# One number per unit instead of a maximum per query: the shift of the scores moves from TensorE into the exponential's bias

## The chip, the cores and the metric

One core of a Trainium2 chip. The metric is device time in microseconds; the kernel before took 1728.9 us (median of 3 runs, 1727.37 to 1731.29). TensorE (PE) multiplies, VectorE (DVE) adds and reduces, ScalarE (ACT) does the exponentials and copies, GpSimd (POOL) issues the adding DMAs, SyncE (SP) issues the other DMAs, each in its own order.

## The reference

A pre-norm block over x of shape (2, 2048, 512): 16 query heads of width 32 in 2 key groups, rotary positions, and then a feed-forward product in emulated 8-bit floats. The part that matters here is the attention:

```python
q = q * cos + rotate_half(q) * sin
q = q * hd ** (-0.5)
k = k * cos + rotate_half(k) * sin
scores = jnp.einsum('bqhd,bkhd->bhqk', q, k_exp) * hd ** (-0.5)
attn = jax.nn.softmax(scores, axis=-1)
out = jnp.einsum('bhqk,bkhd->bqhd', attn, v_exp).reshape(b, s, d)
return out @ wo + bo
```

A softmax is the same whatever number is taken from all scores of one query, as long as the exponentials and their sum stay in range.

## The kernel before, in words

**Units and rounds.** The attention is 64 units of 256 queries by 4 heads. A unit goes over its 2048 keys in 16 chunks of 128, four chunks to a round, so four rounds to a unit (r = 0 to 3). Scores stand as [128 keys, 4 heads x 256 queries] in one of two PSUM tiles `T` (E and O, two banks each); even chunks use one, odd chunks the other. Keys are kept as the difference to the key 256 places earlier (`dkS`), so a chunk's matmuls add to what the tile already holds, and the tile then holds the chunk's own scores.

**A chunk** (`probabilities`, L1008): two matmuls of 512 columns into `T` (L1022), then one exponential of 128x1024 on ACT (L1031) into a tile `p`. Chunk c can start on PE only when the exponential of chunk c - 2 has read the tile.

**The shift before.** For chunks 0 and 1 of a unit, four matmuls of 256 columns (L1013, `sel` against `maxima`) first put minus the maximum of each query into the tile. These maxima come from `first_scores` (L514), called for the next unit at the ends of rounds 0 and 1: four matmuls of 128 columns (L523) give the scores of 128 queries by 128 keys, and DVE reduces them to one maximum per query and head (L531). In round 2 DVE splits the maxima into two parts (L504, L505). In round 3 `gather_maxima` (L538) turns them around with two PE transposes (L543) and copies them to `mT` on ACT (L547).

**The order inside a round** is written out by hand (L1075 on): chunks c0 and c1; DVE adds their two `p` (L1005); PE multiplies the four `p` of the round before with the values (`columns`, L968, 32 matmuls, called by `weigh`); up to two pieces of other work from job queues (`fill`); in round 3 DVE adds two earlier sums (L1038, `join`) and the maxima are gathered; chunks c2 and c3; their DVE addition and a POOL DMA that adds the other pair onto it (L1035); in rounds 0 and 1 `first_scores` of the next unit; one or two more pieces (`fill`), mostly one matmul of a projection (L295) each. The jobs are projections, rotary positions, norms and outputs of other blocks.

**The SP queue** carries the loads of x, keys and queries in program order. A query projection ends in an ACT copy (L439) and, on SP, eight DMAs of 32 KB that swap halves of heads (`sw_q`, L308); the rotated queries are written to DRAM (`q_far`, L469) and read back stacked (`qst`, L349).

**Ends.** `finish_heads` (L934) copies the sums with ACT (L939) and takes their reciprocal as exp(-ln) (L942, L943). At the end of the kernel the largest sum is compared with a bound; if it is over it, or not a number, a slow general path runs (from L1391).

Of the kernel before, what the change touches and what calls it, by code (L numbers as in the profile page):

```python
# [8 lines left out]
F32 = mybir.dt.float32  # L9
F32R = mybir.dt.float32r  # L10
BF16 = mybir.dt.bfloat16
U32 = mybir.dt.uint32
AF = mybir.ActivationFunctionType
ALU = mybir.AluOpType
AX = mybir.AxisListType

P = 128
HEADS = 16
GROUPS = 2
HD = 32  # L20
TB = 512
NT = TB // P
EPS = 1e-5
E4M3_MAX = 448.0
# [3 lines left out]
def preln_attn_fp8_ffn_kernel(  # L28
# [57 lines left out]
    AV_BANKS = 2  # L86
    FIRST = P
    MOST_BITS = float(0x5D5E0B6B)

    const = ctx.enter_context(tc.tile_pool(name="const", bufs=1))  # L90
    xpool = ctx.enter_context(tc.tile_pool(name="x", bufs=3))
# [90 lines left out]
    ones = const.tile([P, HD], F32, tag="ones", name="ones")  # L182
    nc.gpsimd.memset(ones, 1.0)

    sel = const.tile([P, 4, P], F32R, tag="sel", name="sel")
    nc.gpsimd.memset(sel.bitcast(F32), 0.0)
    for j in range(4):
        nc.gpsimd.memset(sel[j * HD : j * HD + 2, j, :].bitcast(F32), -1.0)
    mrow = const.tile([P, HB], F32R, tag="mrow", name="mrow")
    nc.gpsimd.memset(mrow.bitcast(F32), 0.0)  # L190


    def layernorm_stats(src, mean, rstd, name, tiles=range(NT)):
# [17 lines left out]
    def quantized_scale(amax, scale, inv, name):  # L211

        across = bank(f"across_{name}")
        nc.tensor.transpose(across[:1, :P], amax, ident)
        whole = small.tile([1, 1], F32, tag="whole", name=f"whole_{name}")
        nc.vector.tensor_reduce(whole, across[:1, :P], AX.X, ALU.max)
        give_back()
        down = bank(f"down_{name}")

        nc.tensor.matmul(down[:, :1], sel[:1, 0, :].bitcast(F32), whole, start=True, stop=True)  # L220
        nc.vector.tensor_scalar(scale, down[:, :1], -1.0 / E4M3_MAX, 1e-12, ALU.mult, ALU.max)
        give_back()
        nc.vector.reciprocal(inv, scale)

# [269 lines left out]
    def group(k):  # L494
        return quads[k][1] // (QUADS // GROUPS)

    split = []
    largest = {}

    def split_maxima():  # L500

        if split:
            mview, mx = split.pop()
            nc.vector.tensor_copy(mview[:, :, :, 0], mx)  # L504
            nc.vector.tensor_tensor(  # L505
                mview[:, :, :, 1], mx, mview[:, :, :, 0].bitcast(F32), ALU.subtract
            )

    def first_scores(u, i):  # L514

        k, half = units[u]
        if i == 0:
            largest[u] = small.tile([P, HT, 4], F32, tag="mx", name=f"mx_{u}")
        mx = largest[u]
        s = ps_s.tile([P, 4, FIRST], F32, tag="s0", name=f"s_{u}_{i}")  # L520
        at = (half * HT + i) * P
        for j in range(4):
            nc.tensor.matmul(  # L523
                s[:, j, :],
                qst[k][:, j, at : at + P],
                stacked["dkS"][:, group(k), :FIRST],
                start=True,
                stop=True,
                skip_group_check=True,
            )  # L530
        nc.vector.tensor_reduce(mx[:, i, :], s, AX.X, ALU.max)  # L531
        if i == HT - 1:
            mview = mrow.rearrange("p (i j r) -> p i j r", i=HT, j=4)
            split.append((mview, largest.pop(u)))

    maxima = {}

    def gather_maxima(u):  # L538

        split_maxima()  # L540
        tp = ps_s.tile([P, TB], F32, tag="s0", name=f"mtp_{u}")
        for i in range(HT):
            nc.tensor.transpose(  # L543
                tp[:, i * P : (i + 1) * P], mrow[:, i * P : (i + 1) * P].bitcast(F32), ident
            )
        mT = wide.tile([P, HB], F32R, tag="mT", name=f"mT_{u}")
        nc.scalar.copy(mT, tp[:, :HB])  # L547
        maxima[u] = mT


    mean2 = const.tile([P, NBLK, NT], F32, tag="mean2", name="mean2")
# [123 lines left out]
    def run(steps):  # L675
        for _ in steps:
            pass
# [14 lines left out]
    def first(steps, n):  # L692

        for _ in range(n):
            if next(steps, "end") == "end":
                return
            yield
# [4 lines left out]
    with tc.manual_schedule():  # L702
# [22 lines left out]

        run(first(kv[3], FRONT))
        run(prepare_weight(w_all))
        for i in range(HT):
            first_scores(0, i)
        run(first(kv[3], MIDDLE))  # L730
        gather_maxima(0)
        run(kv[3])


    attending[0] = True
# [70 lines left out]
        return 2 if r >= 2 and owed > (ROUNDS + r - 2) * left else 1  # L806

    seen = const.tile([P, len(units)], F32, tag="seen", name="seen")
    without_x = {}
    x_res = {}  # L810
    x_taken, x_done = [], set()
# [111 lines left out]
    def ask(u):  # L923

        k, half = units[u]
        n, quad = quads[k]
        if n == NBLK - 1 and quad == 3 and half == 0:

            fetch_y(4, wide, "qst", bufs=2)
            fetch_y_over_keys(5, "dkS", 0)  # L930
# [3 lines left out]
    def finish_heads(u, both, sums):  # L934
# [4 lines left out]
        nc.scalar.activation(total, sums, AF.Copy, accum_out=seen[:, u : u + 1])  # L939
        yield LATER  # L940
        yield ON_DVE
        nc.scalar.activation(guess, total, AF.Ln)  # L942
        nc.scalar.activation(guess, guess, AF.Exp, scale=-1.0)  # L943
        yield LATER
# [63 lines left out]
    def probabilities(u, T, kc):  # L1008

        k, half = units[u]  # L1010
        if kc < 2:
            for j in range(4):
                nc.tensor.matmul(  # L1013
                    T[:, j, :],
                    sel[:, j, :],
                    maxima[u],
                    start=(j % 2 == 0),
                    stop=True,
                    skip_group_check=True,
                )  # L1020
        for j in range(0, 4, 2):
            nc.tensor.matmul(  # L1022
                T[:, j : j + 2, :],
                stacked["dkS"][:, group(k), kc * P : (kc + 1) * P],
                qst[k][:, j : j + 2, half * HB : (half + 1) * HB],
                start=False,
                stop=True,
                skip_group_check=True,
            )
        p = ppool.tile([P, 4, HB], F32, tag="p", name=f"p_{u}_{kc}")  # L1030
        nc.scalar.activation(p, T, AF.Exp, scale=SCALE)  # L1031
        return p

    def accumulate(to, of):
# [23 lines left out]
    with tc.manual_schedule():  # L1058
        behind = None
        before = None  # L1060
        for u, (k, half) in enumerate(units):
# [13 lines left out]
            for r in range(ROUNDS):  # L1075
# [3 lines left out]
                    landing.pop()()  # L1079
                if r == 2:  # L1080
                    ask(u)
                load_wanted(u)
                load_some()
                last = r == ROUNDS - 1
# [13 lines left out]
                        Job(finish_heads(before.u, before.both, before.avs[:, 1, :]))  # L1098
                    )
                fill(ON_DVE, 2)  # L1100
                if r == 2:
                    split_maxima()
                if last:
                    join(unit.far[1], unit.far[0])
                    if u + 1 < len(units):
                        gather_maxima(u + 1)

                probs.append(probabilities(u, banks[0], chunks[2]))
                probs.append(probabilities(u, banks[1], chunks[3]))
# [4 lines left out]
                if before and r == 1 and in_two(before.u):  # L1114
                    join(before.far[3], before.far[2])
                behind = unit, chunks, probs
                if r < HT and u + 1 < len(units):
                    first_scores(u + 1, r)
                fill(ON_PE, pieces(u, r, ending_soon))
                fill(ON_DVE, 2)  # L1120
# [78 lines left out]
            multiplied(n, i, ready)  # L1199
            ready = ahead  # L1200

    top = small.tile([P, 1], F32, tag="top", name="top")
    nc.vector.tensor_reduce(top, seen.bitcast(U32), AX.X, ALU.max)
    across = bank("across_seen")
    nc.tensor.transpose(across[:1, :P], top, ident)
    flag = small.tile([1, 1], mybir.dt.int32, tag="flag", name="flag")
    nc.vector.tensor_reduce(top[:1], across[:1, :P], AX.X, ALU.max)
    nc.vector.tensor_scalar(flag, top[:1], MOST_BITS, None, ALU.is_gt)
    over = nc.values_load(flag, min_val=0, max_val=1)


# [259 lines left out]
```

## Time and profile before

| what | value |
| --- | --- |
| runs | 1728.9 us median (1727.37 to 1731.29) |
| the profiled execution's own time | 1724.88 us |
| its span | 1723.0 us |
| mean granted TensorE clock | 0.975 |
| exponentials (L1031) | 1024, 992.6 us busy, 1024 ns each |
| `sel` matmuls (L1013) | 512, 94.5 us busy |
| matmuls of the first scores (L523) | 512, 72.8 us busy |
| transposes of the maxima (L543) | 128, 28.0 us busy |
| reductions of the first scores (L531) | 128, 87.5 us busy |

The span runs from the profiled execution's first instruction to its last. A group's busy time is the union of its instructions; matmuls overlap in the pipeline, so that their mean duration is longer than the pitch at which they are issued. "Idle before" is the time for which the engine stood still just ahead of the group, with what ended it. PE is its matmuls and PEld its weight loads; SPq is SP issuing DMAs.

### The profile page before, as it was taken

To read this page: it belongs to the slowest core of one execution; us is meant where nothing else is said; L and a number is where in the kernel's file an instruction comes from. 1 tells how busy PE (TensorE), PEld (TensorE's weight loads), DVE (VectorE), ACT (ScalarE), POOL (GpSimd) and SP (SyncE) were. 2 spreads that over 40 slices of the span, in tenths; PEclk is the share of its full clock that TensorE was granted. 3 is DMA by queue.
4 is the path that set the end of the run, shared out by engine and by line. 5 is a ranking of instruction groups with operands and counts; after the bars stand their busy time and mean duration, and the time that the engine had idled before them with its cause. 6 is when DMAs were issued, how large, how long until landed. Compare 5 with 4: busy or idle time off the path is not lost.

```text
span 1723.0 us, 33241 instructions
## 1 busy us (share of the span) xinstructions
PE 1575.1 (91%) x13483; PEld 900.6 (52%) x13483; DVE 1248.8 (72%) x1673; ACT 1236.4 (72%) x1629; POOL 317.1 (18%) x381
## 2 busy tenths in 40 slices
PE   5499999999999999999999999999999989999565
PEld 2255555555555555555555555555555555555222
DVE  4447677677887769776877687767777686676697
ACT  2257877777777777777777777877777777777375
POOL 3321112211212112211221122111211122111100
PEclk9699999999999999999999999999999999999888
DMA  6657769867778767878786688656867597576222
GB/s 203 201 122 178 170 146 216 195 127 160 184 178 164 183 153 160 192 147 195 175 196 134 118 199 177 152 117 154 184 149 154 105 203 145 116 187 138 56 86 112
DMA packets 105810, 272.61 MB, mean 158 GB/s; under 512 B 15920, under 2 KB 16560, under 8 KB 102960
## 3 DMA queue, kind: packets, MB, share of 16 engines
q0 software_dynamic: 41328, 142.10, 44.2%
q1 hardware_dynamic: 61904, 126.92, 25.3%
q8 instruction: 108, 1.77, 0.4%
q10 hardware_dynamic: 2416, 1.38, 0.3%
q14 instruction: 54, 0.44, 0.1%
HBM read 87.36 MB, written 40.89 MB: 74 GB/s over the span
## 4 chain that ended last, share of the span: by engine, by line
PE 67%; DVE 10%; DMA 8%; issue 7%; ACT 5%; SPq 2%; POOL 1%; ACTq 0%; DVEq 0%; POOLq 0%
PE avs L968 23%; PE T L1022 23%; PE po L295 5%; ACT p L1031 5%; PE pq L295 4%; PE T L1013 3%; PE avs L986 3%; PE s L523 2%; DMA pa<-pa 2%; DMA qst<-q_far 2%; PE pk L295 2%; PE mtp L543 1%; DVE v L236 1%; DVE pa L1005 1%; DMA sw_q<-q 1%
## 5 line engine op out<-in xcount | busy, mean ns | idle before, releaser
L1031 ACT ACTIVATE p<-T 128x1024 f32<-128x1024 f32 x1024 | 992.6, 1024 | 178.3 <-PE T L1022 171.1
L1005 DVE TENSOR_TENSOR pa<-p,p 128x1024 f32<-128x1024 f32 x511 | 624.7, 1223 | 356.1 <-ACT p L1031 355.0
L1022 PE MATMUL T<-qst,dkS 128*128 128x512 f32 x2048 | 680.0, 442 | 24.8 <-ACT p L1031 23.8
L968 PE MATMUL avs<-p,vX 128*32 128x256 f32 x8192 | 495.1, 382 | 0.0
L1022 PEld LDWEIGHTS T<-qst,dkS 128*128 128x128 f32 x2048 | 338.7, 188 | 273.6 <-ACT p L1031 153.5
L1035 POOL DMA_DIRECT2D pa<-pa x255 | 221.0, 867 | 1201.2 <-DVE pa L1005 915.3
L968 PEld LDWEIGHTS avs<-p,vX 128*32 128x32 f32 x8192 | 239.9, 109 | 225.8 <-issue 93.9
L1038 DVE TENSOR_TENSOR pa<-pa,pa 128x1024 f32<-128x1024 f32 x125 | 152.3, 1219 | 16.0 <-DMA pa<-pa 15.9
L295 PE MATMUL po<-wo_sb,attn 128*128 128x512 f32 x256 | 129.6, 603 | 0.0
L295 PE MATMUL pq<-xnT_q,wq_sb 128*128 128x512 f32 x224 | 111.8, 601 | 0.0
L1013 PE MATMUL T<-mT,sel 128*128 128x256 f32 x512 | 94.5, 307 | 6.5 <-ACT p L1031 6.1
L1013 PEld LDWEIGHTS T<-mT,sel 128*128 128x128 f32 x512 | 72.9, 188 | 46.9 <-ACT p L1031 30.8
L986 PE MATMUL avs<-pa,ones 128*32 128x256 f32 x1048 | 80.7, 382 | 11.9 <-DVE pa L1038 11.1
L531 DVE TENSOR_REDUCE mx<-s 128x4 f32<-128x512 f32 x128 | 87.5, 683 | 2.8 <-PE s L523 2.8
L1056 ACT COPY both<-avs 128x256 f32<-128x256 f32 x64 | 23.9, 373 | 86.7 <-PE avs L986 86.7
L523 PEld LDWEIGHTS s<-dkS,qst 128*128 128x128 f32 x512 | 77.2, 192 | 14.7 <-DVE mx L531 3.1
L939 ACT ACTIVATE both<-avs 128x256 f32<-128x256 f32 x64 | 24.6, 385 | 71.7 <-PE avs L986 71.7
L523 PE MATMUL s<-dkS,qst 128*128 128x128 f32 x512 | 72.8, 265 | 2.2 <-DVE mx L531 2.1
L295 PEld LDWEIGHTS po<-wo_sb,attn 128*128 128x128 f32 x256 | 44.3, 190 | 17.6 <-issue 11.0
L986 PEld LDWEIGHTS avs<-pa,ones 128*32 128x32 f32 x1048 | 27.8, 109 | 43.7 <-DVE pa L1038 30.4
L295 PEld LDWEIGHTS pq<-xnT_q,wq_sb 128*128 128x128 f32 x224 | 39.4, 190 | 17.4 <-issue 13.5
L1171 PE MATMUL xtp<-ident_bf,xq 128*128 128x128 bf16 x128 | 16.0, 266 | 34.3 <-DVE xq L237 34.3
(128 smaller groups left out, 1033.0 us busy)
## 6 DMA issues: line engine op xcount, KB each, us to landing
pa<-pa POOLq DMA_DIRECT2D x255, 512.0 KB, 5.2
qst<-q_far SPq DMA_DIRECT2D x128, 256.0 KB, 7.0
q_far<-hi_q SPq DMA_DIRECT2D x32, 256.0 KB, 4.6
q_far<-lo_q SPq DMA_DIRECT2D x32, 256.0 KB, 4.5
x_res<-in_L_attn_x_dram SPq DMA_DIRECT2D x16, 512.0 KB, 10.8
x_res<-in_L_attn_bo_dram POOLq DMA_DIRECT2D x32, 256.0 KB, 6.7
out_dram<-v SPq DMA_DIRECT2D x16, 512.0 KB, 2.8
sw_q<-q SPq DMA_DIRECT2D x240, 32.0 KB, 3.1
```

Of the source, the lines that this page charges most:

```text
L295: nc.tensor.matmul(dst, lhs(c), rhs(c), start=(c == 0), stop=(c == chunks - 1))
L523: nc.tensor.matmul(s[:, j, :], qst[k][:, j, at : at + P], stacked["dkS"][:, group(k), :FIRST], start=True, stop=True, skip_group_check=True,)
L531: nc.vector.tensor_reduce(mx[:, i, :], s, AX.X, ALU.max)
L939: nc.scalar.activation(total, sums, AF.Copy, accum_out=seen[:, u : u + 1])
L968: nc.tensor.matmul(av[j * HD : (j + 1) * HD, :], vX[batch(k)][:, kc, group(k), :], p[:, j, :], start=(kc == 0), stop=(kc == NTS - 1), tile ...
L986: nc.tensor.matmul(dst[j * HD : (j + 1) * HD, :], ones, part[:, j, :], start=start and i == 0, stop=stop and i == len(parts) - 1, tile_pos ...
L1005: nc.vector.tensor_tensor(pa, a, b, ALU.add)
L1013: nc.tensor.matmul(T[:, j, :], sel[:, j, :], maxima[u], start=(j % 2 == 0), stop=True, skip_group_check=True,)
L1022: nc.tensor.matmul(T[:, j : j + 2, :], stacked["dkS"][:, group(k), kc * P : (kc + 1) * P], qst[k][:, j : j + 2, half * HB : (half + 1) * H ...
L1031: nc.scalar.activation(p, T, AF.Exp, scale=SCALE)
L1035: nc.gpsimd.dma_start(out=to, in_=of, accum_op=ALU.add)
L1038: nc.vector.tensor_tensor(to, to, of, ALU.add)
```

## The change

One shift for the whole unit, the largest of its scores at the first 128 keys, is handed to the exponential as its bias. `first_scores` now multiplies with the keys stationary, one matmul of 512 columns in each of rounds 0 and 1, and DVE reduces each result to one number per partition. To bring 128 x 2 numbers together, they are written to DRAM (`put_largest`, start of round 2) and read back to all partitions (`fetch_largest`, start of round 3, 1 KB per partition); DVE reduces them to one number and scales it (`make_shift`, in round 3 after `join`, in the place of `gather_maxima`). The `sel` matmuls, the transposes, the split and the copy to `mT` go. `finish_heads` gets a DVE reduction to the smallest sum (`least`), and the check at the end also looks for sums under 2^-60. The diff, without the constants and the final check:

```diff
     def first_scores(u, i):
         k, half = units[u]
         if i == 0:
-            largest[u] = small.tile([P, HT, 4], F32, tag="mx", name=f"mx_{u}")
...
-        for j in range(4):
-            nc.tensor.matmul(
-                s[:, j, :],
-                qst[k][:, j, at : at + P],
-                stacked["dkS"][:, group(k), :FIRST],
...
-        nc.vector.tensor_reduce(mx[:, i, :], s, AX.X, ALU.max)
+            largest[u] = small.tile([P, 2], F32, tag="mx", name=f"mx_{u}")
+        s = ps_s.tile([FIRST, 2, HB], F32, tag="s0", name=f"s_{u}_{i}")
+        nc.tensor.matmul(
+            s,
+            stacked["dkS"][:, group(k), :FIRST],
+            qst[k][:, 2 * i : 2 * i + 2, half * HB : (half + 1) * HB],
+            start=True,
+            stop=True,
+        )
+        nc.vector.tensor_reduce(
+            largest[u][:, i : i + 1], s.rearrange("p j t -> p (j t)"), AX.X, ALU.max
+        )
+    def put_largest(u):
+        far = dram.tile([P, 2], F32, tag=f"largest_{u % 2}", name=f"largest_{u}")
+        nc.sync.dma_start(far, largest.pop(u))
+        largest_far[u] = far
+    def fetch_largest(u):
+        every = wide.tile([P, 2 * P], F32, tag="every", name=f"every_{u}")
+        nc.sync.dma_start(
+            every, largest_far.pop(u).rearrange("p e -> (p e)").partition_broadcast(P)
+        )
+        shift[u] = every
+    def make_shift(u):
+        every = shift[u]
+        shift[u] = small.tile([P, 1], F32, tag="shift_u", name=f"shift_{u}")
+        nc.vector.tensor_reduce(shift[u], every, AX.X, ALU.max)
+        nc.vector.tensor_scalar(shift[u], shift[u], -SCALE, None, ALU.mult)
...
     def finish_heads(u, both, sums):
+        nc.vector.tensor_reduce(least[:, u : u + 1], total, AX.X, ALU.min)
         nc.scalar.activation(guess, total, AF.Ln)
...
     def probabilities(u, T, kc):
-        if kc < 2:
-            for j in range(4):
-                nc.tensor.matmul(
-                    T[:, j, :],
-                    sel[:, j, :],
-                    maxima[u],
...
-                start=False,
+                start=kc < 2,
...
-        nc.scalar.activation(p, T, AF.Exp, scale=SCALE)
+        nc.scalar.activation(p, T, AF.Exp, bias=shift[u], scale=SCALE)
...
                 if r == 2:
                     ask(u)
+                    if u + 1 < len(units):
+                        put_largest(u + 1)
+                if r == 3 and u + 1 < len(units):
+                    fetch_largest(u + 1)
                 load_wanted(u)
                 load_some()
...
-                if r == 2:
-                    split_maxima()
                 if last:
                     join(unit.far[1], unit.far[0])
                     if u + 1 < len(units):
-                        gather_maxima(u + 1)
+                        make_shift(u + 1)
...
-                if r < HT and u + 1 < len(units):
+                if r < 2 and u + 1 < len(units):
                     first_scores(u + 1, r)
```

## The prediction

> **What bounds the kernel now.** I read the busy times and the chain of waits first, then the weight loads (PEld) of one ordinary unit in order of time, because they show when PE really starts a chunk, then the groups by form for prices, and last SP's part of one unit.
>
> ```profile
> PE 1575.1 (91%) x13483; PEld 900.6 (52%) x13483; DVE 1248.8 (72%) x1673; ACT 1236.4 (72%) x1629; POOL 317.1 (18%) x381
> ...
> PE 67%; DVE 10%; DMA 8%; issue 7%; ACT 5%; SPq 2%; POOL 1%; ACTq 0%; DVEq 0%; POOLq 0%
> ```
>
> PE carries two thirds of the chain, so work taken from PE looks like time won. The weight loads say where that is so. The unit whose first exponential starts at 1328.91 us:
>
> ```profile
> 1327.67 0.53 PEld L1013 LDWEIGHTS T<-mT,sel 128*128 128x128 f32 x4 [0.63 <-ACT p L1031]
> 1328.12 0.31 PEld L1022 LDWEIGHTS T<-qst,dkS 128*128 128x128 f32 x2
> 1328.58 0.56 PEld L1013 LDWEIGHTS T<-mT,sel 128*128 128x128 f32 x4 [0.15 <-ACT p L1031]
> 1329.07 0.31 PEld L1022 LDWEIGHTS T<-qst,dkS 128*128 128x128 f32 x2
> ...
> 1333.95 0.19 PEld L1022 LDWEIGHTS T<-qst,dkS 128*128 128x128 f32 x1 [0.24 <-ACT p L1031]
> ...
> 1334.80 0.30 PEld L1022 LDWEIGHTS T<-qst,dkS 128*128 128x128 f32 x2 [0.22 <-ACT p L1031]
> ```
>
> Two things are to be seen. At every handover from one round to the next PE waits for ACT: chunk c0 for the exponential of c2, chunk c1 for that of c3 (1333.95 and 1334.80 are round 1). And the first `sel` load at 1327.67 waits for ACT as well. So the kernel alternates: two exponentials in a row bound each handover, PE bounds the rest of each round.
>
> **The change part by part.**
>
> *The `sel` matmuls go.* Four last 0.64 us in the timeline, one of them 0.28 us, so their pitch is (0.64 - 0.28) / 3 = 0.12 us, and a unit's eight cost PE 0.96 us. Next late is ACT: in the unit shown the exponential of c3 ends at 1328.53, and the second main pair, now loaded at 1329.07, could start 0.05 later, at 1328.58; 0.49 us are won. In the trace, the first main load stands 0.51 us behind the freeing exponential in 41 of 63 units, 1.3 us (two more matmuls of filling work) in 22; there all 0.96 comes out. 41 x 0.5 + 22 x 0.96 = 42 us won (bounds 31 and 61: all of the one kind, all of the other).
>
> *The transposes and the copy to `mT` go.* In this unit the transposes start at 1325.65 and the main matmuls behind them at 1325.85: 0.20 us x 64 = 13 us won (bounds 0 and 28.0, the group's busy time). The copy (0.37 us) lies on ACT before an exponential that waits for these matmuls and gives nothing more.
>
> *The first scores.* Four matmuls at 0.11 us become one at 0.23 (the pitch of L1022), but they lie ahead of 1333.95, where PE waits for ACT: nothing, or 0.21 x 128 = 27 us won if that cover went.
>
> *The bias.* The exponential now reads its bias from a tile. The trace has no such exponential, but the same shape with a bias tile and a plain copy:
>
> ```profile
> L439 ACT ACTIVATE q<-pq,bq_sb 128x512 f32<-128x512 f32 x32 | 22.1, 689 | 3.7 <-PE pq L295 3.7
> ...
> L285 ACT COPY xnT_kv<-tp_kv 128x512 f32<-128x512 f32 x32 | 18.9, 590 | 20.8 <-PE tp_kv L282 20.8
> ```
>
> That is 0.10 us for each of 1024 exponentials. In mid-round ACT waits for PE and hides it; at a handover two stand in series, 0.2 us. Handovers into rounds 1 and 2 are all bound by ACT (64 + 64), those into round 3 in about three quarters (48), those into round 0 in the 41 units above: 217 x 0.2 = 43 us lost (bounds 0, hidden throughout, and 102, all on the path).
>
> *The round trip through DRAM.* `make_shift` stands in DVE's order, and the next unit's first exponential waits for it; behind it on DVE is the addition of c2 and c3 with its POOL DMA. In an ordinary unit it comes in time: a reduction L531 ends 8.6 us before that exponential, a write of this kind lands in about 2.7 us (`dkS_far`), a read in about 3.1 us (`sw_q`), each with 0.45 us to issue: 6.7 us, and 0.6 for DVE. But the fetch stands in SP's order, and in the built program seven units have the eight `sw_q` between the put and the fetch. One of them:
>
> ```profile
> 734.39 8.93 SPq L308 DMA_DIRECT2D sw_q<-q  x8
> ...
> 737.36 1.22 DVE L1038 TENSOR_TENSOR pa<-pa,pa 128x1024 f32<-128x1024 f32 x1
> ...
> 740.42 1.97 ACT L1031 ACTIVATE p<-T 128x1024 f32<-128x1024 f32 x2 [1.18 <-PE T L1022]
> ```
>
> SP is free at 743.32; 0.45 + 3.1 + 0.5 later, at 747.3, the shift is there, 6.9 us after the exponential that needs it. PE next needs that tile at 743.55, 2.1 us after the exponential's end, and the other tile 1.6 us after its own; less 0.2 for the two biases I take 1.3 us of cover. As the 0.8 us won before it are then waited away, such a unit costs its lateness less 0.5. Reckoned so from SP's issues, the seven are late by 7.7, 4.8, 5.3, 10.2, 4.5, 5.1 and 6.9 us: 44.5 - 3.5 = 41 us. Nine more, where `sw_k` or a late put stands before the fetch, are late by 1.1 to 2.6, 13.6 in all: 13.6 - 4.5 = 9. Together 50 us lost. Bounds: if the eight issues took their median (588 ns each, 4.7 us), the seven would lose about 3 us less each and the nine nothing, 20; if both transfers took 4.9 us (the 128 KB reads of `dkS`), all would be 4 us later: 16 x 4 more, and 47 ordinary units, now early by about 2.0, late by 2.0 at 1.5 each, 50 + 64 + 70 = 184.
>
> Two rules of the Trainium skill, page "DMA: Bandwidth & Descriptors", pull apart here. Its section "Anatomy of one DMA" puts the fixed part of a DMA (on GpSimd's path) at about 2.0 us plus bytes over 436 GB/s; by it put and fetch would take 4.3 us rather than the rows' 5.8, and as an estimate the 16 late units would gain 0.8 to 1.5 us each. Its section "Queues, rings and completion order" has each DMA engine consume a queue's descriptors in order, and so speaks against the change: the fetch would also wait for loads issued just before it, where `x_res` takes 10.8 us to land. I leave the sum with the rows.
>
> *DVE.* `least` and the reduction of 256 numbers cost about 0.42 us each (L946, same width), the scaling 0.17, and 0.35 of splitting goes: 0.66 us more ahead of the addition of c2 and c3, where DVE stood idle for 1.19 us in the unit above. In about ten units `join` ends behind the exponential (887.10 against 884.61 in the worst); 1 us each, 10 us lost (bounds 0 and 0.66 x 64 = 42). The final check sits on DVE ahead of the last additions and costs nothing.
>
> Sum: -42 - 13 + 43 + 50 + 10 = +48, on the profiled execution's own 1724.9 us: 1773. The runs' median lies 4 us above that execution, so I say 1777.
>
> **The rivals.** *The fetch comes in time* (other side): SP issues faster or DVE has slack, and the 60 of the two last terms shrink to about 3; it decides if the fetch leaves SP 4.5 us before the exponential. For it: SP idles for long stretches. Against: 8.93 us of issues in SP's own order. 1777 - 57 = 1720. *PE is the bound throughout:* had PE no waits for ACT, all removed PE work would count (61 + 28 + 27) and the bias nothing: -116 + 60 = 1673. Against it stand the two waits at each handover. *The round trip is late in all units:* 1777 + 134 = 1911 at its bound, some 1865 between that and the forecast's upper end of 1820. For it: 8 bytes per partition are a form that no row here has. *It does not do what it says:* a unit's smallest sum under 2^-60 would start the general path, milliseconds. From the reference's inputs I work out sums down to 2^-7.5 only.
>
> **How the numbers follow.** The forecast, 1745 to 1820: 0.67. Fetch in time, 1712 to 1732: 0.13, of which 0.08 is faster by over 0.2% and 0.05 within it (0.2% is about what a measurement of this kernel can tell from no change). PE-bound, 1650 to 1712: 0.10, faster. Late everywhere, 1820 to 1911: 0.09. The general path: 0.01. Faster 0.18, same 0.05, slower 0.77. The range 1700 to 1825 leaves out the upper case, the general path and most of the PE-bound case, 0.18; the forecast's own is 1745 to 1820.
>
> **What would show it.** Exponentials at about 1.12 us each; waits of PE's chunk loads for ACT growing from 153.5 us; long idle times of ACT's first exponential of some units, ended by DVE's shift, and of DVE, ended by the fetch, in about 7 to 16 units of the first half; the 41 ordinary units within some 0.2 us of before and the 22 with more filling about 0.6 us shorter. Exponentials still at 1.02 us, or no DVE wait for the fetch, would prove me wrong.

## The result, and the profile after

The changed kernel takes 1925.4 us (median of 4 runs, 1914.09 to 1927.43) against 1729.2 before on the same chips: a ratio of 1.112, 95% interval 1.108 to 1.117. The forecast was 1777 with a range up to 1825: slower, as forecast, but by 196 us instead of 48. The profiled execution took 1926.28 us, its span is 1924.4.

The page of the changed kernel: busy time by engine, the chain of waits by engine, then by line.

```profile
PE 1585.5 (82%) x12454; PEld 821.0 (43%) x12459; DVE 1280.7 (67%) x1740; ACT 1290.8 (67%) x1565; POOL 315.2 (16%) x376
...
DMA 34%; PE 24%; DVE 17%; ACT 11%; issue 8%; SPq 4%; POOL 1%; ACTq 0%; DVEq 0%; POOLq 0%
DMA largest<-mx 16%; DMA every<-largest 15%; ACT p L1016 10%; PE T L1007 10%; PE avs L963 7%; DVE pa L1000 4%; SPq L305 4%; DVE pa L1023 3%; PE po L292 2%; PE pq L292 2%; DVE mx L516 1%; DVE shift L538 1%; DVE v L233 1%; DMA pa<-pa 1%; PE pk L292 1%
```

PE's share of the chain falls from 67% to 24%, and DMA's rises from 8% to 34%. Two transfers, the write of 1 KB (`largest`) and the read of 128 KB (`every`), make up 31% of that chain. Who waited for whom in the changed kernel (us in total, times, longest), from the list of all waits:

```profile
PEld T L1007 <- ACT p L1016: 494.1, 577, 9.2
...
ACT p L1016 <- DVE shift L539: 257.6, 63, 10.7
PE T L1007 <- ACT p L1016: 224.8, 292, 8.8
DVE shift L538 <- DMA every<-largest: 217.9, 63, 8.0
```

The number to read is ACT's count, 63: the shift is late in every unit after the first, not in 16. How it comes late is seen in one ordinary unit, with no `sw_q` near it. These are lines from the changed kernel's instructions in order of time: start, duration, engine, line, and the wait ahead in brackets.

```profile
1493.79 0.87 POOL L1020 DMA_DIRECT2D pa<-pa  x1 [6.10 <-PE T L1007]
...
1494.32 0.68 DVE L516 TENSOR_REDUCE mx<-s 128x1 f32<-128x512 f32 x1
...
1495.03 0.32 SPq L523 DMA_DIRECT2D largest<-mx  x1
...
1500.30 0.32 SPq L529 DMA_DIRECT2D every<-largest  x1
...
1505.32 0.42 DVE L538 TENSOR_REDUCE shift<-every 128x1 f32<-128x256 f32 x1 [2.62 <-DMA every<-largest]
...
1505.77 0.15 DVE L539 TENSOR_SCALAR shift<-shift 128x1 f32<-128x1 f32 x1
...
1506.02 2.12 ACT L1016 ACTIVATE p<-T,shift 128x1024 f32<-128x1024 f32 x2 [2.56 <-DVE shift L539]
```

SP issues the write 0.03 us after the reduction's end at 1495.00, so SP isn't to blame in this unit (in nine others the write is issued 1.0 to 4.5 us after the reduction). From this issue to the next, which waits for the write, 5.27 us pass; from the fetch's issue to DVE 5.02; then 0.70 to the exponential. Together 11.0 us, where the prediction had 8.6 to spend, and ACT stands for 2.56. Over all units the medians are 5.65, 4.52 and 0.70 (worked out from the starts in the trace). The two transfers' own rows, from the list of DMA issues (KB each, median us from issue to landing):

```profile
every<-largest SPq DMA_DIRECT2D x64, 128.0 KB, 4.4
...
largest<-mx SPq DMA_DIRECT2D x64, 1.0 KB, 5.3
```

The rows of the kernel before from which the prediction took its two prices, the write's first:

```profile
dkS_far<-lo_dkS SPq DMA_DIRECT2D x8, 128.0 KB, 2.7
```

```profile
sw_q<-q SPq DMA_DIRECT2D x240, 32.0 KB, 3.1
```

A transfer travels in packets, and the trace has the start and the end of each. The write's 128 packets of 8 bytes tell where its 5.3 us go (medians of 63 units): 2.8 us pass from the issue to the first packet, 0.4 from the first to the end of the last, and 2.1 from there to the landing. The first part goes with POOL's adding DMA, the first line of the unit above. In 53 units SP issued the write 0.5 to 3 us after POOL had begun to issue one; there the first packet came 4.0 us after POOL's beginning, 2.8 after SP's. In the other ten it came 1.0 us after SP's. What holds the packets back isn't shown.

Sorted by the prediction's own classes, ACT's first exponential waited for the shift 50.6 us in the seven units with `sw_q` between write and fetch (predicted lateness 44.5), 31.7 in the nine others that it named (13.6), and 175.3 in the 47 units that it held to be in time. In the same classes DVE stood for the fetch 44.2, 19.9 and 152.8 us, in the last a median of 3.1 each.

### The profile page after: what moved, and what is told of

The parts are those of the page before. It is cut to its first block, busy times and chain, and to the rows that moved or that the text cites. A ratio compares the mean times of both kernels' runs of the same rounds, so it can differ in the third digit from the quotient of the medians.

```text
span 1924.4 us, 31328 instructions
## 1 busy us (share of the span) xinstructions
PE 1585.5 (82%) x12454; PEld 821.0 (43%) x12459; DVE 1280.7 (67%) x1740; ACT 1290.8 (67%) x1565; POOL 315.2 (16%) x376
## 4 chain that ended last, share of the span: by engine, by line
DMA 34%; PE 24%; DVE 17%; ACT 11%; issue 8%; SPq 4%; POOL 1%; ACTq 0%; DVEq 0%; POOLq 0%
DMA largest<-mx 16%; DMA every<-largest 15%; ACT p L1016 10%; PE T L1007 10%; PE avs L963 7%; DVE pa L1000 4%; SPq L305 4%; DVE pa L1023 3%; PE po L292 2%; PE pq L292 2%; DVE mx L516 1%; DVE shift L538 1%; DVE v L233 1%; DMA pa<-pa 1%; PE pk L292 1%
## 5 line engine op out<-in xcount | busy, mean ns | idle before, releaser
L1016 ACT ACTIVATE p<-T,shift 128x1024 f32<-128x1024 f32 x1024 | 1079.2, 1115 | 416.2 <-DVE shift L539 257.6
L1007 PE MATMUL T<-qst,dkS 128*128 128x512 f32 x2048 | 748.2, 472 | 227.3 <-ACT p L1016 224.8
L1007 PEld LDWEIGHTS T<-qst,dkS 128*128 128x128 f32 x2048 | 356.2, 199 | 615.8 <-ACT p L1016 494.1
L538 DVE TENSOR_REDUCE shift<-every 128x1 f32<-128x256 f32 x64 | 26.8, 420 | 217.9 <-DMA every<-largest 217.9
L1023 DVE TENSOR_TENSOR pa<-pa,pa 128x1024 f32<-128x1024 f32 x125 | 152.1, 1217 | 15.9 <-DMA pa<-pa 15.8
L292 PE MATMUL pq<-xnT_q,wq_sb 128*128 128x512 f32 x224 | 122.0, 649 | 0.0
L516 DVE TENSOR_REDUCE mx<-s 128x1 f32<-128x512 f32 x128 | 87.3, 682 | 2.1 <-PE s L509 2.1
L509 PE MATMUL s<-qst,dkS 128*128 128x512 f32 x128 | 58.2, 455 | 0.8 <-DVE mx L516 0.8
L279 PE MATMUL tp_kv<-ident,xn_kv 128*128 128x128 f32 x128 | 22.9, 321 | 27.2 <-DVE xn_kv L260 26.6
L292 PE MATMUL pk<-xnT_kv,wkv_sb 128*128 128x512 f32 x64 | 38.6, 721 | 7.4 <-ACT xnT_kv L282 7.4
L1168 PE MATMUL py<-wT,xqT 128*128 128x512 bf16 x123 | 41.3, 464 | 1.9 <-ACT xqT L1160 1.6
```

Of the source, the lines that this page charges most:

```text
L292: nc.tensor.matmul(dst, lhs(c), rhs(c), start=(c == 0), stop=(c == chunks - 1))
L509: nc.tensor.matmul(s, stacked["dkS"][:, group(k), :FIRST], qst[k][:, 2 * i : 2 * i + 2, half * HB : (half + 1) * HB], start=True, stop=True,)
L516: nc.vector.tensor_reduce(largest[u][:, i : i + 1], s.rearrange("p j t -> p (j t)"), AX.X, ALU.max)
L538: nc.vector.tensor_reduce(shift[u], every, AX.X, ALU.max)
L1007: nc.tensor.matmul(T[:, j : j + 2, :], stacked["dkS"][:, group(k), kc * P : (kc + 1) * P], qst[k][:, j : j + 2, half * HB : (half + 1) * H ...
L1016: nc.scalar.activation(p, T, AF.Exp, bias=shift[u], scale=SCALE)
```

## The experiments

All ratios are to the kernel before, run on the same chip (its medians there lie between 1727.5 and 1729.2, so that times of different experiments are set against each other as they stand); "e1" and so on stand for the first part of a label. Several theories stood at the start. *Latency* (theory 1 in the expectations): the round trip is too slow for the time that it has, in all units; the harm is done by ACT's wait (1a) or by DVE, which stands in its order for the fetch (1b). *Its rivals:* the bias on the exponential costs more than thought (theory 2); PE's granted clock, which falls in the changed kernel, is a good part of the loss (theory 3); or SP's queue, held by the two DMAs, does it.

### e1 and e2: without the round trip, with and without a bias

Both drop the trip and DVE's `make_shift`. e1 gives every exponential one fixed bias tile, e2 gives it none.

```diff
-        put_largest(0)
...
-        fetch_largest(0)
...
-        make_shift(0)
...
-        nc.scalar.activation(p, T, AF.Exp, bias=shift[u], scale=SCALE)
+        nc.scalar.activation(p, T, AF.Exp, bias=flat, scale=SCALE)   # e1
+        nc.scalar.activation(p, T, AF.Exp, scale=SCALE)              # e2
...
-                    if u + 1 < len(units):
-                        put_largest(u + 1)
-                if r == 3 and u + 1 < len(units):
-                    fetch_largest(u + 1)
...
-                    if u + 1 < len(units):
-                        make_shift(u + 1)
```

> The bias stays an operand in a tile, but it is a fixed -12 for all units, and nothing is written to DRAM, read back or reduced to a shift; the first scores and their reductions are still computed, for nothing. Theory 1 (the round trip through DRAM is what costs): all of its waits go, what remains is my sum without the two last terms, 1729 - 42 - 13 + 43 = 1717, between 1700 and 1735. Theory 2 (the bias operand is on the path at every exponential, 1024 x 0.1 us): 1729 - 55 + 102 = 1776, over 1760. The granted clock should be back at 0.97 or more if it fell only because PE stood waiting.

> As e1_fixed_bias, but the exponential has no bias operand at all, so that no shift is taken from the scores. What it shows is the gain of the removed PE work alone: by my sum 1729 - 42 - 13 = 1674 (1655 to 1690). Its distance from e1_fixed_bias is the price of the bias operand: 43 us by my sum, 102 by theory 2, near 0 if ACT has the room.

Measured: e1 1713.9 us (ratio 0.992, 0.989 to 0.995), e2 1684.0 (0.975, 0.972 to 0.977). Both lie in the ranges expected. So the trip and all that waits for it cost 1925.4 - 1713.9 = 211 us, the bias 1713.9 - 1684.0 = 30 (theory 2 had 102), and what is left of the change wins 44. The mean granted clock is back at 0.973. The exponentials and PE's chunk loads (busy, mean ns | idle before, releaser), e1's page first:

```profile
L1015 ACT ACTIVATE p<-T,flat 128x1024 f32<-128x1024 f32 x1024 | 1069.3, 1115 | 150.7 <-PE T L1006 148.8
...
L1006 PEld LDWEIGHTS T<-qst,dkS 128*128 128x128 f32 x2048 | 337.5, 188 | 438.7 <-ACT p L1015 305.7
```

And the exponentials on the page of e2:

```profile
L1013 ACT ACTIVATE p<-T 128x1024 f32<-128x1024 f32 x1024 | 988.9, 1024 | 175.7 <-PE T L1004 169.1
```

The chunk loads in the kernel before:

```profile
L1022 PEld LDWEIGHTS T<-qst,dkS 128*128 128x128 f32 x2048 | 338.7, 188 | 273.6 <-ACT p L1031 153.5
```

One bias operand costs 91 ns (1115 against 1024). The chunk loads' wait for ACT grows from 153.5 us in the kernel before to 250.8 in e2 and, with the bias, to 305.7 in e1: much of the work taken from PE comes back as a wait, as the prediction had it, with a small rest won. e2 is faster than the kernel before by 44 us; it holds only for scores that need no shift.

### e8: the kernel before with a bias of zero

```diff
-        nc.scalar.activation(p, T, AF.Exp, scale=SCALE)
+        nc.scalar.activation(p, T, AF.Exp, bias=flat, scale=SCALE)
```

> The kernel before with one edit: the exponential takes a bias from a tile of zeros. It prices the operand where the sel matmuls still stand. e1_fixed_bias less e2_no_bias gave 30 us. By my sum the handovers into rounds 1 to 3 pay it (176 x 0.2 = 35 us) and those into round 0 hide it behind the sel matmuls: 1728 + 35 = 1763 (1750 to 1765). If each exponential paid on the path, 1830.

Measured: 1758.7 us (1.018, 1.015 to 1.021), 30 us more than before and within the range expected. The page of e8:

```profile
L1033 ACT ACTIVATE p<-T,flat 128x1024 f32<-128x1024 f32 x1024 | 1079.4, 1113 | 150.0 <-PE T L1024 137.5
```

With the `sel` matmuls or without them, the operand costs 30 us, a third of the 93 us by which the 1024 exponentials become longer. The rest lies in ACT's waits for PE.

### e7: no first scores either

On top of e2, the matmuls and reductions of the first scores go.

```diff
-        for i in range(2):
-            first_scores(0, i)
...
-                if r < 2 and u + 1 < len(units):
-                    first_scores(u + 1, r)
```

> No shift at all: no first scores, no reductions, no trip, no bias operand; the sums are still checked at both ends. As e2_no_bias (1684), less two 512-column matmuls and two reductions of 0.68 us on DVE a unit. If first scores lie under ACT's time as I reckoned, 1675 to 1684; if PE bounds the ends of rounds 0 and 1, up to 2 x 0.23 x 64 = 30 us less, 1654.

Measured: 1687.5 us (0.976, 0.973 to 0.978), within 4 us of e2. The new form of the first scores costs nothing that can be measured, on PE or on DVE, as predicted.

### e9 and e3: the trip without its readers, and with DVE alone waiting

e9 issues both DMAs and nobody reads the result (`make_shift` goes). e3 keeps `make_shift`, so that DVE waits for the fetch, but the exponential takes the fixed bias.

```diff
-        make_shift(0)
...
-                    if u + 1 < len(units):
-                        make_shift(u + 1)
...
-        nc.scalar.activation(p, T, AF.Exp, bias=shift[u], scale=SCALE)
+        nc.scalar.activation(p, T, AF.Exp, bias=flat, scale=SCALE)
```

(e3 has the last two lines alone.)

> Put and fetch are issued on SP as in the change, but nobody reads what comes back: no shift on DVE, the fixed -12 as bias. If only waiting for the number costs, this is e1_fixed_bias, 1714 (to 1725). If the trip also costs by holding up SP's queue (SP waits 680 us for the reductions and 246 us for the writes), so that loads behind it come late, it lies over 1740.

> The whole round trip stays, and DVE still waits for the fetch and makes the shift, but the exponential takes the fixed -12, so that ACT no longer waits for it. Theory 1a (ACT's wait of 257.6 us is the path): within 20 us of e1_fixed_bias, about 1735. Theory 1b (DVE standing in its order, 217.9 us, holds everything up through the additions queued behind it): over 1850.

Measured: e9 1732.3 us (1.001, 0.999 to 1.003; 10 runs, 1722.69 to 1737.11), 18 above e1. e3 1823.6 (1.056, 1.053 to 1.059), 110 above e1 and 91 above e9. Both lie between the two values that were expected. SP's own waits in e9:

```profile
SPq L525 <- DVE mx L518: 548.5, 54, 17.8
SPq L531 <- DMA largest<-mx: 242.4, 50, 10.2
```

791 us of standing cost 18 us of time, so most of it falls where SP had nothing urgent behind the wait. The 18 is not sharp: e9's runs spread over 14 us, and the two profiled executions lie 7 us apart (1724.05 and 1717.14). Nor does e9 tell SP's standing from the 128 KB that each fetch moves. Who waited in e3:

```profile
DVE shift L540 <- DMA every<-largest: 183.6, 58, 8.9
...
PE s L511 <- DVE mx L518: 65.0, 26, 4.6
```

DVE's stand alone makes the later reductions of the next unit's first scores late, and PE, which has to reuse their tile, waits 65.0 us for DVE. The rounds show the same place: from the first exponential of round 1 to that of round 2, summed over the units, it is 451.0 us against 365.7 in e1.

### e12: DVE's wait moved to the end of round 3

`make_shift` leaves its place after `join` and is called as the last thing of round 3, so that DVE's additions no longer stand behind it.

```diff
                 if last:
                     join(unit.far[1], unit.far[0])
-                    if u + 1 < len(units):
-                        make_shift(u + 1)
...
+                if last and u + 1 < len(units):
+                    make_shift(u + 1)
```

> The change, with the shift made on DVE at the end of round 3, behind the addition of c2 and c3 and the filling work, so that nothing of this unit stands behind the wait for the fetch. e3_exp_free less e9_trip_unread put 91 us on DVE standing in its order with nobody waiting for the number. If that 91 adds to the wait of the exponential (102 us, the change less e3_exp_free), the time falls to about 1835. If both are one lateness counted at two places (the exponential needs the number at that moment anyway), it stays within 25 us of 1925.

Measured: 1908.5 us (1.101, 1.097 to 1.106), 17 below the changed kernel. In e12:

```profile
ACT p L1016 <- DVE shift L539: 242.4, 61, 9.9
...
DVE shift L538 <- DMA every<-largest: 93.5, 46, 7.0
```

DVE's wait falls from 217.9 to 93.5 us, ACT's hardly (257.6 to 242.4), and so does the time. DVE's stand costs 91 us where it is alone (e3 against e9) and 17 where ACT waits as well: for the most part the two are one lateness, counted at two places, as the second of the two expectations had it, and must not be added.

### e6: the write in rows of 512 bytes

Each partition writes 128 numbers (its two maxima and filling) instead of two; the fetch reads the first two rows, so the shift comes from two keys only. The fetch keeps its size of 1 KB per partition.

```diff
+    wide_mx = [const.tile([P, P], F32, tag=f"mxw{e}", name=f"mxw{e}") for e in range(2)]
...
-            largest[u] = small.tile([P, 2], F32, tag="mx", name=f"mx_{u}")
+            largest[u] = wide_mx[u % 2]
...
-        far = dram.tile([P, 2], F32, tag=f"largest_{u % 2}", name=f"largest_{u}")
+        far = dram.tile([P, P], F32, tag=f"largest_{u % 2}", name=f"largest_{u}")
...
-            every, largest_far.pop(u).rearrange("p e -> (p e)").partition_broadcast(P)
+            every, largest_far.pop(u)[:2, :].rearrange("p e -> (p e)").partition_broadcast(P)
```

> The change, but each partition writes a row of 512 bytes, not 8, and the fetch reads back the rows of the first two partitions, so that the shift is the largest of two keys' scores only; everything else, the waits too, is the same. If the 8-byte rows make the write slow (5.1 us in the median, where 128 KB of dkS land in 2.9), the write falls to about 3 us and each unit is 2 us less late: about 1925 - 120 = 1805. If a write to DRAM and its receipt are slow whatever the rows, it stays within 20 us of 1925.

Measured: 1832.2 us (1.060, 1.058 to 1.063), 93 below the changed kernel, where 120 were expected. DVE's wait, on the page of e6:

```profile
L541 DVE TENSOR_REDUCE shift<-every 128x1 f32<-128x256 f32 x64 | 26.6, 416 | 121.2 <-DMA every<-largest 121.2
```

ACT's, from the list of waits:

```profile
ACT p L1019 <- DVE shift L542: 148.7, 43, 11.8
```

The two transfers, in e6's list of DMA issues:

```profile
every<-largest SPq DMA_DIRECT2D x64, 128.0 KB, 3.7
...
largest<-mxw SPq DMA_DIRECT2D x64, 64.0 KB, 3.6
```

Sixty-four times the bytes land sooner: 3.6 us instead of 5.3. By the packets the gain lies behind the last one: from its end to the landing 0.36 us pass in the median, where the 8-byte write has 2.1. The 2.8 us ahead of the first packet stay as they were. The fetch lands 0.7 sooner as well; by its packets that is mostly time ahead of the first one (1.8 us to 1.2), which points to the moment at which it goes out and not to the two rows. DVE's wait for the fetch falls by 217.9 - 121.2 = 97 us, ACT's for the shift by 109, and the time by 93. This is the most direct support of the latency theory: with the trip shortened and its place and its readers left as they are, the loss shrinks by about as much as the waits. The Trainium skill, page "DMA: Bandwidth & Descriptors", section "Specifications", gives 512 B as the least transfer for full rate and says that a smaller one is done by read-modify-write. The 2.1 us against 0.36 go the same way, but they are a delay and not a rate, and no run here shows the read-modify-write itself.

### e4: the first scores one unit earlier

The first scores of unit u + 2 are made in rounds 2 and 3 of unit u, the write goes out at round 0 and the fetch at round 1 of unit u + 1, two rounds earlier than in the change.

```diff
-                    if u + 1 < len(units):
-                        put_largest(u + 1)
-                if r == 3 and u + 1 < len(units):
+                if r == (2 if u == 0 else 0) and u + 1 < len(units):
+                    put_largest(u + 1)
+                if r == (3 if u == 0 else 1) and u + 1 < len(units):
                     fetch_largest(u + 1)
...
-                if r < 2 and u + 1 < len(units):
+                if r < 2 and u == 0:
                     first_scores(u + 1, r)
+                if r >= 2 and u + 2 < len(units):
+                    first_scores(u + 2, r - 2)
```

> The change whole, but the first scores of a unit are computed one round pair earlier (rounds 2 and 3 of the unit before the last), put at the start of round 0 and fetched at the start of round 1, two rounds ahead of where the change has them; the first two units keep the old places. Theory 1: a trip of 5.3 + 4.4 us and two issues then fits into two and a half rounds (about 14 us); the time is that of e1_fixed_bias plus DVE's 0.6 us a unit where it has no room, 1717 to 1745. If the transfers disturb SP's queue or the other DMAs rather than come late, it stays over 1790.

Measured: 1860.8 us (1.077, 1.073 to 1.081), over the 1790 that was to speak for disturbed transfers. In e4:

```profile
PE s L509 <- DMA qst<-q_far: 100.0, 17, 12.4
...
ACT p L1016 <- DVE shift L539: 27.1, 23, 5.2
```

The trip is now nearly in time: ACT's wait for the shift falls from 257.6 to 27.1 us. But 147 us over e1 remain, 129 of them in round 2, and the largest new wait is PE's for the stacked queries, 100.0 us in 17 units. The earlier first scores need these loads a unit sooner; in the 17 units the last of the four was issued only 7 to 16 us before PE had it. How much of that comes of the write and the fetch ahead of them on SP, and how much of the earlier need alone, isn't told apart. So this experiment shows the latency theory's wait gone and another in its place; it doesn't give the gain of a trip in time.

It shows one thing more, in its list of DMA issues:

```profile
every<-largest SPq DMA_DIRECT2D x64, 128.0 KB, 5.6
...
largest<-mx SPq DMA_DIRECT2D x64, 1.0 KB, 3.6
```

The same write of 8 bytes per partition, issued at the start of round 0, lands in 3.6 us instead of 5.3. Its packets start 0.8 us after the issue and not 2.8; the 2.0 us behind the last one remain. So the size of the pieces and the moment of the issue each make about 1.7 us of the write's 5.3.

### e5 and e11: the number brought together on the chip

No DMA. DVE takes the larger of the two columns, PE transposes it (1 column), DVE reduces the row, PE spreads the one number over the partitions, DVE scales it. In e5 the transpose stands at the end of round 2 and the spreading in the place of `make_shift`; e11 puts the transpose there and the spreading at the end of round 3.

```diff
...
+        one = small.tile([P, 1], F32, tag="one", name=f"one_{u}")
+        nc.vector.tensor_tensor(one, both[:, :1], both[:, 1:], ALU.max)
...
+        tp = ps_s.tile([P, TB], F32, tag="s0", name=f"ltp_{u}")
+        nc.tensor.transpose(tp[:1, :P], largest_far.pop(u), ident)
+        top = small.tile([1, 1], F32, tag="top_u", name=f"top_{u}")
+        nc.vector.tensor_reduce(top, tp[:1, :P], AX.X, ALU.max)
...
+        down = ps_s.tile([P, TB], F32, tag="s0", name=f"ldown_{u}")
+        nc.tensor.matmul(down[:, :1], row, shift[u], start=True, stop=True)
...
+        nc.vector.tensor_scalar(shift[u], down[:, :1], -SCALE, None, ALU.mult)
```

> The change whole, with the numbers brought together on the chip: DVE takes the larger of the two maxima per partition in round 2, PE turns them into one row at the end of round 2, DVE reduces the row, and in round 3 a one-column PE matmul spreads the number to all partitions; nothing goes to DRAM. If the DRAM trip is the whole loss, this is e1_fixed_bias (1714) plus two small PE instructions a unit, about 0.3 us each of which one lies in the part bound by PE, and a little DVE: 1725 to 1750. If any wait for one number per unit ahead of its first exponential is what costs, it stays over 1800.

> As e5_on_chip, with both PE steps later: the row is made in round 3 after join, and the spreading matmul stands at the end of round 3. In e5_on_chip PE waited 35.9 us at the row for a late DVE, and round 2 grew by 39 us over e1_fixed_bias. If that place was the loss, 1725 to 1745. If the exchange itself costs (the exponential then waits for a chain of PE, DVE, PE, DVE through join), it stays at 1765 or more.

Measured: e5 1765.3 us (1.021, 1.019 to 1.024), e11 1779.8 (1.030, 1.027 to 1.033). That is 160 and 146 us less than the change, and 51 and 66 more than e1. e5 misses its lower expectation by 15 us and is far from the upper; e11 lies where the exchange itself was to cost. In e5 PE's transpose waits for DVE:

```profile
PE ltp L530 <- DVE one L524: 35.9, 30, 2.9
```

And in e11 the spreading does, and then ACT for the shift:

```profile
ACT p L1017 <- DVE shift L540: 70.7, 52, 2.9
PE ldown L538 <- DVE top L532: 54.6, 51, 3.6
```

The five steps alternate between DVE and PE, and each stands in the order of an engine that has other work ahead of it. For e5 the 35.9 us of this wait are named; of the other 15 us of its 51 the profile shows no single owner.

### e10: PE kept busy while it waits

In the changed kernel PE's granted clock falls. The stretches of the trace (busy time of the engines, then PEclk, DMA share, GB/s); before first:

```profile
100.00:400.00 300.00, 290.78 (x2568) 169.60 (x2567) 223.00 (x287) 234.45 (x308) 53.16 (x60) 1.00 0.78 173
```

The changed kernel:

```profile
100.00:400.00 300.00, 242.93 (x1921) 130.08 (x1923) 184.01 (x243) 201.42 (x241) 46.66 (x52) 0.91 0.71 152
400.00:700.00 300.00, 266.63 (x2162) 141.91 (x2155) 211.85 (x281) 217.33 (x261) 47.21 (x55) 0.95 0.71 148
```

e10 adds eight matmuls of 512 columns, whose result nobody reads, at the place in round 0 where PE waits.

```diff
+                if r == 0 and before:
+                    idle = ps_s.tile([P, 2, HB], F32, tag="s0", name=f"idle_{u}")
+                    for _ in range(8):
+                        nc.tensor.matmul(
+                            idle,
+                            stacked["dkS"][:, group(k), :FIRST],
+                            qst[k][:, :2, half * HB : (half + 1) * HB],
...
```

> The change, with eight matmuls of 512 columns into an unused PSUM tile in round 0, just before the chunk for which PE waits on the late exponentials (8 x 0.23 = 1.9 us a unit, 118 us in all, into a result that nobody reads). In the change the granted clock fell to a half in 36 stretches of the attention, 177 us in all. Theory 3 (the fallen clock is a good part of the loss): the clock stays at 0.96 or more over the span and the time falls below 1900, since the extra work lies in PE's wait. Theory 1 (the wait alone): the clock may recover, but the time stays within 15 us of 1925 or rises by what of the 118 us finds no wait to lie in.

Measured: 1921.4 us (1.110, 1.107 to 1.114), no change against the changed kernel's 1925.4 that the intervals can tell. The mean clock rises from 0.932 to 0.953. The same stretches of e10:

```profile
100.00:400.00 300.00, 258.49 (x2016) 140.72 (x2016) 185.86 (x246) 203.44 (x242) 45.19 (x51) 0.95 0.72 153
400.00:700.00 300.00, 281.60 (x2257) 154.47 (x2260) 210.80 (x279) 218.00 (x262) 48.04 (x56) 0.98 0.71 148
```

By the trace the clock stands at half for 88 us of the kernel before, 265 of the changed kernel and 182 of e10. The 64 x 8 extra matmuls (118 us at a pitch of 0.23) fit into PE's waits: the chunk loads' wait for ACT falls from 494.1 to 396.7 us.

The unchanged time doesn't show that the fallen clock costs nothing, because e10 gave back only 83 of the 177 us that the change had added, and because the rounds show a balance (worked out from the starts and the clock in the trace). In the changed kernel 34 of the 64 rounds 0 have a stretch at half clock. In 16 of these e10 has none, and all 16 are shorter there, by 0.3 to 1.6 us, 18.9 in all. One of them, the changed kernel first:

```profile
1109.53:1115.66 6.13, 4.69 (x10) 2.84 (x11) 5.55 (x8) 4.51 (x6) 0.91 (x2) 0.72 0.45 86
```

```profile
1107.71:1112.21 4.50, 4.23 (x16) 2.23 (x14) 3.92 (x6) 4.41 (x6) 0.87 (x1) 1.00 0.44 85
```

What was won there is lost elsewhere: the 30 rounds 0 with the full clock in both kernels are 13.8 us longer together in e10, where the extra matmuls stand in them, and its rounds 3, where the shift is late, 15.9. So the fallen clock follows from the waits and lengthens the rounds after them: at 1.2 us for each of the 34 rounds by some 40 us, an estimate. How much of that would be won by the full clock alone no run shows.

## Why the prediction was right in sign and wrong in size

The runs give the terms one by one, each the difference of two medians taken against the kernel before on the same chip:

| term | predicted us | measured us | from |
| --- | --- | --- | --- |
| `sel`, transposes, first scores; `least` and the split included | -55 (and some of +10) | -44 | e2 to before |
| bias | +43 | +30 | e1 to e2, e8 to before |
| SP held by the two DMAs | nothing | +18 | e9 to e1 |
| the shift late, with what the fallen clock costs | +50 | +193 | changed kernel to e9 |
| sum | +48 | +197 (196 measured at once) | |

**Wrong: "In an ordinary unit it comes in time".** This is the step that failed. It took the write at 2.7 us, from `dkS_far`, and the read at 3.1, from `sw_q`, 6.7 with the issues, against 8.6 available. The write landed in a median of 5.3 us and the read in 4.4. The write's row differed in two things that mattered. A DMA to `dkS_far` writes 128 KB, the one to `largest` 1 KB in 128 pieces of 8 bytes, and e6 shows larger pieces alone to land 1.7 us sooner. And the write goes out at a moment, 1.2 us after POOL's adding DMA in most units, at which its packets start late; e4 shows the same 8-byte pieces at another moment to land 1.7 us sooner. The rows of `dkS_far` could have warned of the second: six of their sixteen writes (`hi` and `lo`) ran ahead of the attention, in 2.2 to 3.2 us, and the ten in it took 2.3 to 5.3, a median of 3.3. The prediction wrote that "8 bytes per partition are a form that no row here has" and set both transfers at 4.9 us as its upper bound. With 9.7 together the truth stood at that bound (9.8), and the bound's price for the trip, 184, was near the measured 193 (211 with SP's part). That it came so near is in part luck, since the 4.9, taken for both, was the row of other reads. The rival *late in all units* was thus the case that happened, at its bound of 1911 and some 14 over; a chance of 0.09 for it and a range that stopped at 1825 were the second error. With a margin of under 2 us in an ordinary unit and a price without a row of its form, the margin was smaller than the doubt in the price.

**Also wrong: the page weighed against the rows.** The prediction set beside the rows' 5.8 us the 4.3 that follow from the Trainium skill, page "DMA: Bandwidth & Descriptors", section "Anatomy of one DMA"; measured were 9.7. The page states its fixed part for GpSimd's path, and SP issues these two, so the rows don't refute the page; as an estimate for this pair it was much too low, and the measurement decides. The order in a queue, which the prediction set against the change, is not isolated by any run; in keeping with it, DVE stood 4.6 to 5.8 us in the four units in which SP issues `x_res` loads between the write and the fetch.

**Mis-sized: the cover.** The prediction let 1.3 us of each lateness vanish. Between e1 and the changed kernel, summed over the units, round 3 up to the next unit's first exponential grows by 255 us, and the rounds 0, 1 and 2 give back 33, 12 and 6: 0.8 us a unit. The difference goes with the clock: the 30 rounds 0 at full clock give back all of the 33 us, 1.1 each, and the 34 with a stretch at half clock nothing.

**Left out: SP's queue.** The prediction looked at what stands ahead of the fetch and not at what stands behind the two waits. That is 18 us in e9, as far as they are SP's.

**Right.** Of the signs that the prediction named, the exponentials at 1.12 us, the growing wait of the chunk loads (153.5 to 494.1 us) and the idle times ended by the shift and by the fetch all came, these in 63 units instead of 7 to 16. In the seven units with `sw_q` between write and fetch ACT waited 50.6 us, 44.5 forecast. ACT bounds the handovers: e1 shows PE's wait for ACT doubled, so only 44 us came out of the 137 us of busy time that PE lost (94.5 + 72.8 + 28.0 for `sel`, first scores and transposes before, less 58.2 for the new first scores). The first scores cost nothing (e7). The bias costs part of its 0.1 us: 30 us of 93, 43 predicted. Without the trip's terms the prediction's own sum is -42 - 13 + 43 = -12, with up to 10 for DVE, or 1717 to 1727 from the median before; e1 took 1713.9. DVE's +10 has no run of its own: `least` and the missing split are in the -44, `make_shift` in the +193.

**Open:** the trace shows where the write's time goes, 2.8 us ahead of its packets and 2.1 behind them, but not what holds it there. What the fallen clock costs is an estimate. How fast the change would be with the shift in time isn't measured either: e4 brought it in time and paid elsewhere. From e9, without DVE's two steps, it would be about 1732, and from e1 1714 if SP weren't held.

## What to carry to other kernels

Price a DMA by a row of its own bytes per partition and of the stage in which it will run; if there is none, compare the margin with the doubt in the price, and where the margin is smaller, let the range reach the late case in all units. A small exchange that must be ready at a fixed point costs its lateness on every turn, at whichever engine waits first, and taking one engine's wait away leaves the other's: 17 us were won without DVE's (e12), 102 of 193 without ACT's (e3). Shorten the transfer or do without it: here the version without any shift was the fastest, at 1684.0 us (for scores that need none), and the exchange on the chip cost 51 us over a fixed bias. Work taken from an engine that waits at a handover counts only up to the next wait, 44 us here of 137.

## What the runs showed of the hardware

- The 128 x 8 B write to DRAM on SP's queue took a median of 5.3 us to land, the 128 x 512 B write 3.6, at a DMA share of 0.68 to 0.79 (changed kernel) and 0.72 to 0.76 (e6). From the end of its last packet to the landing the first took 2.1 us, the second 0.36.
- Where SP issued that write 0.5 to 3 us after POOL had begun to issue an adding DMA (53 of 63 units of the changed kernel), its first packet came 4.0 us after POOL's beginning; in the other ten 1.0 us after its own issue. In e6 the medians are the same, and in e4, where most writes go out 0.1 us after POOL's beginning, it is 0.8.
- A bias read from a tile makes a 128x1024 exponential 91 ns longer (1024 to 1115).
- PE's granted clock, 1.00 in all five stretches from 100 to 1600 us before, was 0.91 to 0.96 there in the changed kernel; it falls to half for 3.4 us or a multiple of it at a time (43 of 44 stretches). Sixteen rounds 0 that had such a stretch in the changed kernel and none in e10 were 18.9 us shorter in e10.
